# Layer-1 state-space decays: differences of running sums over 24 rows instead of 128-row sums of steps

## The chip, the cores and the metric

The kernel runs on one core of one Trainium2 chip. The metric is device time in microseconds (us) of one execution. The kernel before took 3012.22 us, the median of 18 runs (3007.47 to 3018.83).

## What is computed

The program is a whole decoder of four layers over 32 sequences of 64 tokens (2048 tokens, width 256). Each layer has an attention-like mixer, a cross attention and a feed-forward part. The change touches one of the twelve parts: the mixer of layer 1, a state-space model with 32 heads. Layer 2 has a mixer of the same kind with 8 heads, in the same functions. Cut to what matters, the reference for layer 1 is:

```python
dt = softplus(dt + dt_bias)
A = -exp(A_log)                         # one negative number for each head
dA = exp(dt * A)
def step(h, inp):                       # one step for each token of a sequence
    h = dA_t[:, :, None, None] * h + (dt_t[:, :, None] * x_t)[..., None] * B_t[:, :, None, :]
    y = einsum('bhpn,bhn->bhp', h, C_t)
```

The kernel doesn't walk over the tokens. Over a sequence of 64 tokens the recursion is a masked product: token n adds to the output of token m (m not before n) its input dt·x, weighted by C·B of the two tokens and by a decay, exp(da[n+1] + ... + da[m]) with da = dt·A. All da are negative. So for each head there is a 64x64 matrix of decays, and what the change replaces is how the exponents of these matrices are summed.

## The kernel before, in words

**Tiling.** The tokens lie in 16 tiles of 128 rows; a tile holds two whole sequences. A unit of the mixer (`unit_ssm`, line 1369) takes two tiles, 256 tokens. It normalizes, projects dt and computes da (lines 1380 to 1389; da is 128 rows by 2 tiles by 32 heads), and prepares B, C and their masked product cb. Then `unit_ssm_heads` (line 1401) runs four times for layer 1, with j = 0, 4, 8 and 12, eight heads each (once for layer 2). Such a call is called a block below. Layer 1 has 8 units, so 32 blocks; layer 2 has 8 units, so 8 blocks.

**A block before.** One elementwise product makes `ra` (lines 1411 to 1414): the step da of a row, repeated over 64 columns, kept where the column's token is at or after the row's (`upto`). It is recorded with `combine`, which lets the planner choose VectorE or GpSimd. For each of the two tiles, one matmul of the constant 128x128 matrix `after` with 512 columns of `ra` (line 1421) sums the steps between two tokens, and ScalarE's Exp takes the sum out of PSUM into `m` (line 1422). VectorE multiplies m by cb (line 1423). The rest of the block are the projections and the four-tap convolution (`pair`, `conv`), transposes, 32 small 64x64 products of inputs and decays, the gate, and the output projection, which accumulates in two PSUM banks over the four blocks of a unit.

**Engines.** A float32 matmul shows in the trace as two instructions, each with its weight load. TensorE's array is split when a product has few rows or columns: a product over 32 rows uses one of four row strips (the start partition, 0, 32, 64 or 96, says which). `cross_out` (line 1175) uses all four strips at once.

**The order of the work.** The functions only record operations. A planner (`Order`, line 531, and `in_turns`, line 777) puts them in order for each engine before the program is built: a list scheduler that runs forward and backward in turns and keeps the shortest of its forward plans by its own cost formulas (`duration`, line 467). For TensorE these formulas give a float32 product over 128 rows and 512 columns 0.86 us, and one over at most 32 rows 512 x 0.00053 = 0.27 us; a switch between shapes costs 0.1 us (`SWITCH`). While TensorE is in a split shape, ready products of the same shape that stand near (within 10 us of work, `NEAR`) are preferred. Two streams of stages are woven in one order (`body`, line 2568), in three groups of 8, 6 and 2 tiles, so that layer-1 blocks of a later group stand beside stages of layers 2 and 3 of an earlier one. Buffers come from fixed numbers of slots: ten of 4 KB a row (`b4`, where `ra` lies), sixteen of 2 KB (`b2`), eight PSUM banks (`mm`).

Of the kernel before, what the change touches and what calls it, by code (L numbers as in the profile page):

```python
# [22 lines left out]
AF = mybir.ActivationFunctionType  # L23
ALU = mybir.AluOpType
AX = mybir.AxisListType

P = 128
# [14 lines left out]
def _constants():  # L42

    f = np.float32
    r = np.arange(P)
    c = {}
    c["ident"] = np.eye(P, dtype=f)
    c["ones"] = np.ones((P, P), f)

    c["causal"] = np.where(np.arange(64)[None, :] <= (r % 64)[:, None], 0.0, NEG).astype(f)  # L50

    c["upto"] = ((r % 64)[:, None] <= np.arange(64)[None, :]).astype(f)

    c["after"] = ((r[:, None] > r[None, :]) & (r[:, None] // 64 == r[None, :] // 64)).astype(f)

    c["before"] = (r[:, None] < r[None, :]).astype(f)

    c["strip8"] = ((r[:, None] % 32) // 8 == np.arange(4)[None, :]).astype(f)
    c["strip16"] = ((r[:, None] % 32) // 16 == np.arange(2)[None, :]).astype(f)

    c["parity"] = (r[:, None] // 64 == np.arange(2)[None, :]).astype(f)

    c["unit"] = np.broadcast_to(np.eye(1, 32, dtype=f), (P, 32))
    c["iota"] = np.broadcast_to(np.arange(64, dtype=f), (P, 64))
    main = ((r % 64) < 48).astype(f)
    c["mainT"] = np.zeros((P, P), f)
    c["mainT"][0], c["mainT"][1] = main, 1 - main
    c["row"] = r[:, None].astype(f)

    at = (np.arange(NT)[:, None, None] * P + r[None, :, None]) * 6 + np.arange(6)[None, None, :] - NONE  # L70
    c["parts"] = np.transpose(at, (1, 0, 2)).reshape(P, NT * 6).astype(f)
    c["mhalf"] = np.full((P, 32), -0.5, f)

    inv = f(1.0) / f(500000.0) ** (np.arange(0, 64, 2, dtype=f) / f(64))
    ang = inv[r % 32][:, None] * np.arange(64, dtype=f)[None, :]
    co, si = np.cos(ang).astype(f), np.sin(ang).astype(f)
    c["rope0"] = np.concatenate([co, np.where(r[:, None] // 32 % 2 == 0, -si, si)], 1)
    inv = f(1.0) / f(10000.0) ** (np.arange(0, 8, 2, dtype=f) / f(8))
    ang = (r % 64).astype(f)[:, None] * inv[None, :]
    co, si = np.cos(ang).astype(f), np.sin(ang).astype(f)  # L80
    c["rope3"] = np.concatenate([co, co, -si, si], 1)
    at, parts, n = {}, [], 0
    for k, v in c.items():
        at[k] = (n, n + v.shape[1])
        n += v.shape[1]
        parts.append(v.astype(f))
    return np.ascontiguousarray(np.concatenate(parts, 1)), at


_CONST, _AT = _constants()  # L90


# [110 lines left out]
def bc(ap, axis, n):  # L203

    u = ap.unsqueeze(axis)
    s = list(u.shape)
    s[axis] = n
    return u.broadcast_to(s)
# [11 lines left out]
def split(ap, a, pat="p (a b) -> p a b"):  # L220
    return ap.rearrange(pat, a=a)
# [572 lines left out]
class Net:  # L794
# [41 lines left out]
    def k(self, name):  # L836
        a, b = _AT[name]
        return self.const[:, a:b]

    def tile(self, tag, *shape, dtype=F32, parts=P):  # L840
        self.n += 1
        name = sys._getframe(1).f_code.co_name
        if name in ("w", "w4", "b4", "b2", "tmp", "sm", "mm"):
            name = sys._getframe(2).f_code.co_name
        name = f"{name.removeprefix('unit_')}_{tag}_{self.n}"
        t = Tile(tag, [parts, *shape], dtype, name, "psum" if tag == "mm" else "sbuf")
        dims, n = [], 1
        for c in reversed(shape):
            dims.insert(0, (n, c))
            n *= c  # L850
        return View(t, 0, parts, 0, dims, dtype)
# [517 lines left out]
    def unit_ssm(self, layer, W, nh, g, st):  # L1369

        nc = self.nc
        nx = nh // 2
        wx, wg, wr, wo, par = W
        cw = par["cw"].rearrange("p (c k) -> p c k", k=4)
        upto = self.k("upto")
        hT = self.norm(layer, [2 * g, 2 * g + 1])
        pre = self.tile("pre", 256)
        dt, da, cb = (split(pre[:, a : a + 2 * n], 2) for a, n in ((0, nh), (64, nh), (128, 64)))

        pd = split(self.mm()[:, : 2 * nh], 2)  # L1380
        for t in range(2):
            self.prod(pd[:, t, :], [(hT[:, c, t * P : (t + 1) * P], wr[:, c, 256:]) for c in range(2)])
        e = self.sm(2, nh)
        nc.vector.tensor_tensor(dt, pd, bc(par["dtb"], 1, 2), ALU.add)
        nc.scalar.activation(e, dt, AF.Abs)
        nc.scalar.activation(e, e, AF.Exp, scale=-1.0)
        nc.scalar.activation(e, e, AF.Ln, bias=1.0)
        nc.vector.scalar_tensor_tensor(dt, dt, 0.0, e, ALU.max, ALU.add)
        nc.vector.tensor_tensor(da, dt, bc(par["alog"], 1, 2), ALU.mult)
        BC = self.tmp(2, GT)  # L1390
        self.conv(par, cw, BC, self.pair([wr[:, c] for c in range(2)], 0, hT), nx)

        pc = split(self.mm()[:, :P], 2)
        for t in range(2):
            for b in range(2):
                at = slice(t * P + b * 64, t * P + b * 64 + 64)
                nc.tensor.matmul(pc[64 * b : 64 * b + 64, t, :], BC[:, 0, at], BC[:, 1, at], start=True, stop=True)
        nc.vector.tensor_tensor(cb, pc, bc(upto, 1, 2), ALU.mult)
        st.update(hT=hT, dt=dt, da=da, cb=cb)

    def unit_ssm_heads(self, W, nh, g, j, st):

        nc = self.nc
        nx = nh // 2
        wx, wg, wr, wo, par = W
        cw = par["cw"].rearrange("p (c k) -> p c k", k=4)
        upto = self.k("upto")
        first, last = j == 0, j + 4 == nx
        hT, dt, da, cb = st["hT"], st["dt"], st["da"], st["cb"]

        ra = self.b4(2, 8, 64)
        nc.combine(
            ra, bc(da[:, :, 2 * j : 2 * j + 8], 3, 64), bc(bc(upto, 1, 2), 2, 8), ALU.mult
        )
        xs = self.b4(4, GT)
        for u in range(0, 4, 2):
            self.conv(par, cw, xs[:, u : u + 2, :], self.pair(wx, (j + u) * P, hT), j + u)
        gs, m = self.b4(4, GT), self.b4(2, 8, 64)
        for t in range(2):
            ps = self.mm()  # L1420
            self.prod(ps, [(self.k("after"), ra[:, t])])
            nc.scalar.activation(m[:, t], split(ps, 8), AF.Exp)
        nc.vector.tensor_tensor(m, m, bc(cb, 2, 8), ALU.mult)
        for u in range(0, 4, 2):
            nc.scalar.activation(gs[:, u : u + 2, :], self.pair(wg, (j + u) * P, hT), AF.Silu)
# [1 line left out]
        for t in range(2):  # L1427
            ps = split(self.mm(), 4)
# [39 lines left out]
        for u in range(4):  # L1468
            if u == 3:
                for v in range(4):  # L1470
                    rows = slice(32 * v, 32 * v + 32)
# [1140 lines left out]
```

## Time and profile before

The profiled execution took 3022.26 us; its span on the core is 3020.5 us.

| | |
|---|---|
| median of 18 runs | 3012.22 us |
| profiled execution / its span | 3022.26 / 3020.5 us |
| mean granted TensorE clock | 0.961 |
| TensorE matmul (PE) busy | 2850.1 us, 94% |
| VectorE (DVE) | 2110.1 us, 70% |
| GpSimd (POOL) | 1554.6 us, 51% |
| ScalarE (ACT) | 1509.0 us, 50% |
| HBM traffic | 85 GB/s over the span |

Every instruction has the same line in this profile (L2503, the helper that issues the plan), so the groups are told apart by tiles: `ssm_heads_b` and `ssm_heads_mm` are SBUF and PSUM tiles of a block, `ssm_pre` holds dt, da and cb of a unit, `__init___consts` the constants. A form such as 32*128 32x512 is a matmul that uses 32 rows and 128 columns of the array and streams 512 columns. Matmuls overlap, so the time that a matmul takes from the stream is the distance from its start to the next one's start, and not the duration in its row.

The layer-1 mixer's units stand in three stretches of the span: four units from about 442 to 762 us, three from 1462 to 1772, one from 2318 to 2420.

### The profile page before, as it was taken

The page shows a single profiled execution, that of the slowest core. Times are in us where ns is not written, and L with a number is a line of the kernel's source. Part 1 is how long each engine was busy: PE and PEld are TensorE (multiplying, and loading weights), DVE is VectorE, ACT ScalarE, POOL GpSimd, SP SyncE. Part 2 cuts the span into 40 slices and gives each one's busy share as a digit, 9 for nine tenths or more (in the row PEclk, how much of TensorE's full clock was granted, in tenths as well). Part 3 has the DMA queues.
Part 4 walks back from the last instruction along what each step waited for, and adds up shares of the span by engine and source line. Part 5 has one row for each costly group of instructions (what it writes and reads, how often), then busy time and mean ns, then how long its engine had stood idle before and what let it go on. Part 6 is the DMA issues. An engine that isn't in the chain of part 4 may idle for free.

```text
span 3020.5 us, 66624 instructions
## 1 busy us (share of the span) xinstructions
PE 2850.1 (94%) x26612; PEld 2355.5 (78%) x26612; DVE 2110.1 (70%) x5110; ACT 1509.0 (50%) x2842; POOL 1554.6 (51%) x1323
## 2 busy tenths in 40 slices
PE   8999999999998999999999999998899999987667
PEld 7888888777787888888887788777778788866446
DVE  5773548766677667765899987777457889877434
ACT  5552226565444454634666656654326565664330
POOL 6761243234655455326674566665333685465445
PEclk8999999999999999999999999998999999988878
DMA  4012511301531344121010010123561231212424
GB/s 166 16 47 84 181 58 29 138 2 46 211 137 43 93 163 156 54 70 46 29 34 28 26 44 16 69 79 112 192 222 50 73 103 52 87 36 76 139 90 132
DMA packets 120313, 258.90 MB, mean 86 GB/s; under 512 B 27077, under 2 KB 81880, under 8 KB 107588
## 3 DMA queue, kind: packets, MB, share of 16 engines
q1 hardware_dynamic: 110212, 230.54, 22.5%
q0 software_dynamic: 9792, 24.10, 2.3%
q8 instruction: 211, 3.46, 0.5%
q14 instruction: 98, 0.80, 0.1%
HBM read 179.24 MB, written 78.77 MB: 85 GB/s over the span
## 4 chain that ended last, share of the span: by engine, by line
PE 52%; DVE 6%; issue 3%; ACT 2%; POOL 1%; another core or an unknown queue 0%; POOLq 0%; ACTq 0%; DVEq 0%
PE L_xattn_mm L2503 7%; PE pair_mm L2503 6%; PE ssm_heads_mm L2503 5%; PE cross_out_mm L2503 5%; PE L_ffn_mm L2503 4%; PE L_attn_mm L2503 3%; PE L_block_mm L2503 3%; PE turn_mm L2503 2%; PE heads_mm L2503 2%; PE L_dense_mm L2503 2%; PE L_experts_mm L2503 2%; PE small_scores_mm L2503 2%; PE outrows_mm L2503 1%; PE L_expert_mm L2503 1%; PE small_values_mm L2503 1%
## 5 line engine op out<-in xcount | busy, mean ns | idle before, releaser
L2503 PE MATMUL pair_mm<-norm_b,load_ssm_w 128*128 128x256 f32 x1280 | 304.5, 381 | 1.4 <-ACT ssm_heads_b L2503 0.8
L2503 PEld LDWEIGHTS pair_mm<-norm_b,load_ssm_w 128*128 128x128 f32 x1280 | 236.3, 190 | 40.8 <-issue 8.3
L2503 DVE SCALAR_TENSOR_TENSOR ssm_heads_b<-pair_mm,load_ssm_wp,ssm_heads_b 128x252 f32<-128x252 f32 (+2 forms) x480 | 196.4, 465 | 26.0 <-ACT ssm_heads_b L2503 24.7
L2503 POOL TENSOR_TENSOR L_xattn_sm<-L_xattn_sm,__init___consts 128x8 f32<-128x8 f32 (+2 forms) x64 | 188.1, 2944 | 26.0 <-DVE L_xattn_sm L2503 19.8
L2503 POOL TENSOR_TENSOR norm_sm<-norm_sm,__init___consts 128x1 f32<-128x1 f32 (+1 forms) x149 | 94.7, 641 | 207.0 <-DVE norm_sm L2503 177.7
L2503 ACT ACT_TABLE_LOAD x151 | 193.7, 1283 | 9.2 <-PE ssm_heads_mm L2503 2.8
L2503 ACT COPY rope_b<-rope_mm 32x512 f32<-32x512 f32 x238 | 137.0, 576 | 121.8 <-DVE rope_b L2503 78.9
L2503 ACT COPY L_xattn_b<-L_xattn_mm 128x512 f32<-128x512 f32 x170 | 99.9, 591 | 163.8 <-PE L_xattn_mm L2503 149.8
L2503 PE MATMUL rope_mm<-norm_b,load_L_attn_w 128*128 128x128 f32 x1280 | 169.3, 289 | 5.1 <-ACT rope_b L2503 3.0
L2503 PEld LDWEIGHTS rope_mm<-norm_b,load_L_attn_w 128*128 128x128 f32 x1280 | 161.8, 203 | 12.8 <-issue 6.3
L2503 PE MATMUL ssm_heads_mm<-load_ssm_w,ssm_heads_b 128*128 128x256 f32 x640 | 165.2, 391 | 0.2 <-POOL ssm_heads_b L2503 0.2
L2503 ACT COPY turn_b<-turn_mm 128x512 f32<-128x512 f32 x192 | 106.1, 595 | 76.1 <-PE turn_mm L2503 71.6
L2503 PEld LDWEIGHTS ssm_heads_mm<-load_ssm_w,ssm_heads_b 128*128 128x128 f32 x640 | 115.9, 191 | 33.5 <-issue 18.4
L2503 POOL TENSOR_TENSOR rope_b<-rope_b,__init___consts 128x512 f32<-128x512 f32 x74 | 82.3, 1113 | 99.4 <-ACT rope_b L2503 71.0
L2503 ACT COPY norm_b<-norm_mm 128x256 f32<-128x256 f32 (+1 forms) x139 | 58.7, 437 | 143.2 <-PE norm_mm L2503 118.9
L2503 DVE TENSOR_SCALAR norm_b<-__init___x,norm_sm,norm_sm 128x256 f32<-128x256 f32 x192 | 110.1, 590 | 26.4 <-POOL norm_sm L2503 10.7
L2503 PEld LDWEIGHTS L_xattn_mm<-norm_b,load_L_xattn_w 128*128 128x128 f32 x1024 | 120.3, 192 | 7.7 <-issue 6.1
L2503 POOL TENSOR_TENSOR ssm_heads_b<-ssm_heads_b,ssm_heads_b 128x1024 f32<-128x1024 f32 x33 | 80.5, 2444 | 88.4 <-DVE ssm_heads_b L2503 64.2
L2503 PE MATMUL cross_out_mm<-load_L_xattn_w,cross_out_b 128*128 128x256 f32 x512 | 124.5, 389 | 0.0
L2503 PE MATMUL L_xattn_mm<-norm_b,units_L_xattn_w 128*128 128x128 f32 x1024 | 121.8, 276 | 2.8 <-issue 2.8
L2503 PE MATMUL L_xattn_mm<-norm_b,load_L_xattn_w 128*128 128x128 f32 x1024 | 124.3, 276 | 0.0
L2503 POOL TENSOR_TENSOR L_xattn_b<-L_xattn_b,shift_sm 128x1024 f32<-128x1024 f32 x30 | 58.1, 1937 | 128.3 <-DVE shift_sm L2503 108.3
(434 smaller groups left out, 7954.2 us busy)
## 6 DMA issues: line engine op xcount, KB each, us to landing
L_block_w<-in_f_rows SPq DMA_DIRECT2D x42, 770.0 KB
queue<-far_w SPq DMA_DIRECT2D x14, 1024.0 KB
load_ssm_w<-in_s_in SPq DMA_DIRECT2D x12, 1024.0 KB
parts<-far_w SPq DMA_DIRECT2D x10, 1024.0 KB
slots<-far_w SPq DMA_DIRECT2D x16, 548.0 KB
L_experts_b<-slots SPq DMA_DIRECT2D x32, 274.0 KB
units_L_xattn_w<-kept_x SPq DMA_DIRECT2D x8, 1024.0 KB
L_parts_b<-parts SPq DMA_DIRECT2D x14, 512.0 KB
```

Of the source, the lines that this page charges most:

```text
L2503: done = getattr(getattr(nc, e), method)(*map(real, op.args), **kw)
```

## The change

For layer 1 alone (nx == 16), the exponent is made as a difference of running sums. Once for a unit, da is spread over 128 columns (four strips of 32: in a strip 8 heads in each of four kinds: first sequence, second sequence, both, none), and for each tile one matmul of this spread with 192 constant columns (`upto` and `within`) gives the running sums. Two tiles are then built from the sums in PSUM: `lo` (128 rows by 2 by 128) and `hi` (128 rows by 2 by 8 by 64, a `b4` slot). In a block j, the product over rows 8j to 8j+24 of `lo` and `hi` is running sum at m minus running sum at n: 24 rows, in strip j/4. The two products of a block lie in the same strip; the four blocks of a unit lie in four different strips. Above the diagonal the difference has the wrong sign and could be large, so ScalarE takes it from PSUM with Relu of the negated value, and a third activation makes the exponentials of all 1024 columns from SBUF. Layer 2's blocks stay as they were. The cost formulas of the planner and the stages' costs are unchanged.

```diff
+    c["within"] = ... # 128 columns
+    c["kinds"] = ...  # 4
+    c["side"] = ...   # 128
+    c["floor"] = ...  # 2
+    c["own"] = ...    # 8
...
 unit_ssm
         nc.vector.tensor_tensor(da, dt, bc(par["alog"], 1, 2), ALU.mult)
+        rows = None
+        if nx == 16:
+            sp = self.tmp(2, 4, 4, 8)
+            for t in range(2):
+                nc.vector.tensor_tensor(
+                    sp[:, t], bc(split(da[:, t], 4), 2, 4), bc(bc(self.k("kinds"), 1, 4), 3, 8), ALU.mult
+                )
+            pc = self.mm()[:, :384].rearrange("p (t n) -> p t n", t=2)
+            for t in range(2):
+                self.prod(pc[:, t], [(sp[:, t].rearrange("p a b c -> p (a b c)"), self.both("upto", "within"))])
+            lo, hi = self.tmp(2, P), self.b4(2, 8, 64)
+            fl = self.k("floor")
+            nc.vector.scalar_tensor_tensor(lo, pc[:, :, 64:], fl[:, 1:2], bc(self.k("side"), 1, 2), ALU.mult, ALU.add)
+            for t in range(2):
+                nc.vector.scalar_tensor_tensor(
+                    hi[:, t], bc(pc[:, t, :64], 1, 8), fl[:, 0:1], bc(self.k("own"), 2, 64), ALU.max, ALU.mult
+                )
+            rows = lo, hi
...
 unit_ssm_heads
-        ra = self.b4(2, 8, 64)
-        nc.combine(
-            ra, bc(da[:, :, 2 * j : 2 * j + 8], 3, 64), bc(bc(upto, 1, 2), 2, 8), ALU.mult
-        )
+        rows = st["rows"]
+        if not rows:
+            ra = ... # as before
...
             ps = self.mm()
-            self.prod(ps, [(self.k("after"), ra[:, t])])
-            nc.scalar.activation(m[:, t], split(ps, 8), AF.Exp)
+            if rows:
+                r = slice(8 * j, 8 * j + 24)
+                self.prod(ps, [(rows[0][r, t], rows[1][r, t].rearrange("p h n -> p (h n)"))])
+                nc.scalar.activation(m[:, t], split(ps, 8), AF.Relu, scale=-1.0)
+            else:
+                ... # as before
+        if rows:
+            nc.scalar.activation(m, m, AF.Exp, scale=-1.0)
         nc.vector.tensor_tensor(m, m, bc(cb, 2, 8), ALU.mult)
```

The new constants add 270 columns to a tile of 1145 that is loaded at the start.

More of the change, by code (lines that the diff above doesn't have):

```diff
@@ L52, in _constants @@
     c["upto"] = ((r % 64)[:, None] <= np.arange(64)[None, :]).astype(f)
+    kind = r[:, None] % 32 // 8
+    half = np.arange(P)[None, :] // 64
+    c["within"] = np.where((r[:, None] // 64) == half, (r[:, None] % 64) <= (np.arange(P)[None, :] % 64), False).astype(f)
     c["after"] = ((r[:, None] > r[None, :]) & (r[:, None] // 64 == r[None, :] // 64)).astype(f)
+    c["kinds"] = np.concatenate([r[:, None] < 64, r[:, None] >= 64, r[:, None] >= 0, r[:, None] < 0], 1).astype(f)
+    c["side"] = ((kind == half) & (kind < 2)).astype(f)
+    c["floor"] = np.concatenate([np.where(kind == 2, 1.0, -3e38), np.where(kind == 2, -1.0, 0.0)], 1).astype(f)
+    c["own"] = ((r[:, None] % 8 == np.arange(8)[None, :]) & (kind < 3)).astype(f)
     c["before"] = (r[:, None] < r[None, :]).astype(f)
@@ L838, in k, with both @@
         return self.const[:, a:b]
+    def both(self, a, b):
+        return self.const[:, _AT[a][0] : _AT[b][1]]
     def tile(self, tag, *shape, dtype=F32, parts=P):
@@ L1398, in unit_ssm @@
         nc.vector.tensor_tensor(cb, pc, bc(upto, 1, 2), ALU.mult)
-        st.update(hT=hT, dt=dt, da=da, cb=cb)
+        st.update(hT=hT, dt=dt, da=da, cb=cb, rows=rows)
     def unit_ssm_heads(self, W, nh, g, j, st):
@@ L1409, in unit_ssm_heads @@
         hT, dt, da, cb = st["hT"], st["dt"], st["da"], st["cb"]
-        ra = self.b4(2, 8, 64)
-        nc.combine(
-            ra, bc(da[:, :, 2 * j : 2 * j + 8], 3, 64), bc(bc(upto, 1, 2), 2, 8), ALU.mult
-        )
+        rows = st["rows"]
+        if not rows:
+            ra = self.b4(2, 8, 64)
+            nc.combine(
+                ra, bc(da[:, :, 2 * j : 2 * j + 8], 3, 64), bc(bc(upto, 1, 2), 2, 8), ALU.mult
+            )
         xs = self.b4(4, GT)
@@ L1420, in unit_ssm_heads @@
             ps = self.mm()
-            self.prod(ps, [(self.k("after"), ra[:, t])])
-            nc.scalar.activation(m[:, t], split(ps, 8), AF.Exp)
+            if rows:
[3 more added lines that the diff above has]
+            else:
+                self.prod(ps, [(self.k("after"), ra[:, t])])
+                nc.scalar.activation(m[:, t], split(ps, 8), AF.Exp)
+        if rows:
+            nc.scalar.activation(m, m, AF.Exp, scale=-1.0)
         nc.vector.tensor_tensor(m, m, bc(cb, 2, 8), ALU.mult)
```

## The prediction

> **What bounds the kernel now.** I read the totals and the slices first, then the three stretches where the layer-1 mixer runs, then the chain of waits in the weakest of them, then groups by form, then single rows of the timeline.
>
> ```profile
> PE 2850.1 (94%) x26612; PEld 2355.5 (78%) x26612; DVE 2110.1 (70%) x5110; ACT 1509.0 (50%) x2842; POOL 1554.6 (51%) x1323
> 442.00:762.00 320.00, 319.17 (x2717) 256.50 (x2716) 223.98 (x546) 186.12 (x296) 116.86 (x79) 1.00 0.14 51
> 1462.00:1772.00 310.00, 306.90 (x3123) 248.91 (x3123) 280.60 (x709) 197.93 (x355) 177.45 (x148) 1.00 0.11 35
> 2318.00:2420.00 102.00, 102.00 (x934) 80.58 (x934) 80.40 (x194) 64.45 (x120) 63.41 (x39) 1.00 0.19 66
> ```
>
> The last three are the stretches of the 4, 3 and 1 layer-1 units: length, then busy time of PE, PEld, DVE, ACT and POOL, the granted clock (1.00), DMA share and GB/s. TensorE is busy for 728 of 732 us, so in these stretches a microsecond of TensorE work is a microsecond of the kernel, and work of ScalarE (about 61%) and GpSimd is covered. VectorE is covered in the first and third stretch (70 and 79%); in the second it has 90%, and the chain of waits there runs partly over it:
>
> ```profile
> by line: PE pair_mm L2503 25.2%; PE ssm_heads_mm L2503 19.8%; PE L_xattn_mm L2503 5.4%; DVE fp_b L2503 5.4%; PE turn_mm L2503 4.3%; POOL L_xattn_sm L2503 4.0%; DVE ssm_heads_b L2503 3.8%; PE small_values_mm L2503 3.7%; PE L_attn_mm L2503 3.
> ```
>
> So TensorE decides, and the question is what a 24-row product costs against one of 128 rows.
>
> **The main products.** Timeline rows (start, length, engine, instructions):
>
> ```profile
> 475.44 1.88 PE L2503 MATMUL ssm_heads_mm<-ssm_heads_b,__init___consts 128*128 128x512 f32 x4
> 477.16 0.38 PE L2503 MATMUL L_ffn_mm<-load_L_ffn_w,L_ffn_b 128*128 128x256 f32 x1
> ...
> 2960.72 2.11 PE L2503 MATMUL L_dense_mm<-norm_b,load_L_experts_w 128*128 128x256 f32 x9
> 2962.75 2.85 PE L2503 MATMUL L_dense_mm<-L_dense_b,d_L_experts_w 32*128 32x256 f32 x12
> 2965.53 1.13 PE L2503 MATMUL L_dense_mm<-load_L_ffn_ws,L_ffn_b 64*128 64x256 f32 x4
> ...
> 269.83 2.02 PE L2503 MATMUL cross_out_mm<-blocks_b,context_cx 32*128 32x512 f32 x16
> ```
>
> The first is a block's pair of products now: 4 instructions, 477.16 - 475.44 = 1.72 us to the next start, 0.43 us each; 32 blocks take 55 us. In the second group 9 full-array instructions of 256 columns take 2.03 us to the next start, 12 in one 32-row strip 2.78 us: 0.226 and 0.232 us each. **Rows that aren't used save nothing: a strip streams its columns as slowly as the whole array.** Only the last row shows a gain: 16 instructions of 512 columns in 2.02 us, with four strips at work, where 16 x 0.43 would be 6.9. The change puts both products of a block in one strip, so a block alone still takes 1.72 us.
>
> The Trainium skill ("TensorE: Matmul & The Clock Gate", section "Why this matters for your kernels") states that a single product over 32 rows takes as long as one over 128, and that only products in distinct row groups run together, 3.07 times as fast for four. By its factor, with four strips always filled, the 55 us would shrink by an estimated 37 us; by its first half they don't shrink at all. The strip rows above agree with that first half.
>
> **What the split shape adds.** By the first group 256 columns take 0.43 / 2 = 0.215 us, so the nine take 1.94 of their 2.03 us and 0.09 goes into changing shape; the twelve take 2.58 of 2.78, and 0.20 goes. One visit to the split shape costs 0.29 us. If each block makes one visit, 32 x 0.29 = +9.3 us. Bounds: 0 (beside another split shape, where the change is paid already) and twice that, if the two tiles' products are issued apart.
>
> **The sums once for a unit.** 2 products x 2 instructions x 192 columns, at 0.43/512 us a column: 0.65 us, x 8 units = +5.2 us of TensorE.
>
> **What strips may give back.** The strips of a unit are filled at once only if products of two blocks stand side by side. All eight of a unit can start as soon as lo and hi are there, and the order now does bring blocks near each other:
>
> ```profile
> 600.41 1.02 PE L2503 MATMUL ssm_heads_mm<-ssm_heads_b,__init___consts 128*128 128x512 f32 x2
> 601.27 0.60 PE L2503 MATMUL ssm_heads_mm<-__init___consts,ssm_heads_b 128*128 128x128 f32 x4
> 601.71 1.02 PE L2503 MATMUL ssm_heads_mm<-ssm_heads_b,__init___consts 128*128 128x512 f32 x2
> 602.57 0.59 PE L2503 MATMUL pair_mm<-norm_b,load_ssm_w 128*128 128x256 f32 x2
> 603.16 1.10 PE L2503 MATMUL ssm_heads_mm<-ssm_heads_b,__init___consts 128*128 128x512 f32 x2
> ```
>
> Three products in 3.6 us; one more follows at 608.33. In each of the first four units two of the four blocks come within some 10 us, and the planner prefers a near product of the same split shape. I take one meeting of two blocks for each unit: 8. A meeting saves one visit (0.29) and between nothing and all of the second block's 1.72 us: each strip's own products go one after the other, and how far the second strip runs ahead in the queue no row shows. I take half, 0.86: 8 x 1.15 = -9.2 us. Bounds: 0 meetings, and 16 (every block meets another) with full overlap, 16 x 2.01 = -32.
>
> TensorE in sum: 9.3 + 5.2 - 9.2 = **+5.3 us**.
>
> **The other engines.**
>
> ```profile
> L2503 POOL TENSOR_TENSOR ssm_heads_b<-ssm_pre,__init___consts 128x1024 f32<-128x1024 f32 x34 | 67.2, 1985 | 86.3 <-PE ssm_heads_mm L2503 35.1 <-DVE ssm_heads_b L2503 17.6 <-DVE ssm_pre L2503 15.5
> L2503 ACT ACTIVATE ssm_heads_b<-ssm_heads_mm 128x512 f32<-128x512 f32 x80 | 44.6, 597 | 18.7 <-PE ssm_heads_mm L2503 18.3
> L2503 ACT ACTIVATE heads_b<-heads_b 128x1024 f32<-128x1024 f32 x64 | 67.1, 1065 | 12.2 <-POOL heads_b L2503 10.9 <-DVE heads_b L2503 1.1
> ```
>
> - Removed: 32 of `ra`, 29 on GpSimd (the row above holds layer 2's too): 29 x 1.985 = 57.6 us, and 3 on VectorE. GpSimd isn't the bound; nothing is gained directly.
> - VectorE added for a unit: two spreads (128 elements; `ssm_pre<-ssm_mm` of that size 0.28 us), lo (the 128x256 `__init___x<-ssm_heads_mm`, 0.476 us) and two halves of hi (512 from PSUM: 0.682 us for a product of two, some 0.07 more with a scalar operand, as 0.476 stands to 0.411 at 256): 2.54 us, x 8 = 20.3 us.
> - ScalarE: two Relu of the size that the two Exp had (0.597 us), plus one Exp of 1024 from SBUF: 1.065 x 32 = 34 us more. No Relu is in the trace; Identity stands between two Silu there without a table load (455.4 to 457.5 us), so I take none for Relu. With two loads a block, 2 x 1.283 us, ScalarE would have 10% more to do, still covered.
> - Of these, what counts is the second stretch: VectorE 3 x 2.54 = 7.6 us and ScalarE 12 x 1.065 = 12.8 us, 20.4 together. Its 12 `ra` were all on GpSimd, so VectorE saves none there. 13.2% of the chain there is named as VectorE's or GpSimd's: **+2.7 us**. Bounds: -6.5 (a VectorE product of 1024 takes 1.75 us beside a GpSimd one and 1.22 alone; 12 x 0.54 comes back) and +20.4.
> - The multiply by cb now waits for Relu and a longer Exp. Behind it on VectorE stand the next convolution steps, and TensorE waits for m in the 64x64 products; with 728 of 732 us busy it has other work then. Nothing taken; it is in the +20.4.
> - hi holds one of ten `b4` slots for a whole unit (some 60 us); `ra` held one four times for a unit (three made at 515.9 to 519.6 us were used from 521 to 564). I take no difference.
> - The first GpSimd step waits for the constants, issued at 1.20 us and landed at 5.66. 270/1145 = 24% more bytes: **+0.7 us**, bounds 0 and 1.05. No DMA is moved past another.
>
> **Sum:** 5.3 + 2.7 + 0.7 = +8.7 us. The profiled execution took 3022.3 (span 3020.5, 1.8 around it), 10 above the median of the runs; on it 3031.0, on the median 3012.2 + 8.7 = **3021 us**.
>
> **Rivals.**
>
> *Strips filled (faster).* Every block meets another and fully overlaps: 9.3 + 5.2 - 32 + 3.4 = -14 us, 2998. For it: the products are all ready at once and near ones are preferred. Against it: a free PSUM bank for each (two of eight hold the output sums), and 20 us of other work between two blocks in the first stretch (320 us / 16).
>
> *No strips meet.* 9.3 + 5.2 + 3.4 = +18 us, 3030. For it: transposes and projections lie between the products in the rows above. The change then doesn't do what a product over strips is for.
>
> *The second stretch turns to VectorE (slower).* Price: all of the 20.4 us, with meetings as in my forecast: 5.3 + 20.4 + 0.7 = +26 us, 3039. It decides once VectorE's idle time there (310 - 281 = 29 us) can't take the added 20 us of it and ScalarE's longer chain. Against it: TensorE is idle for only 3 us there now.
>
> **Chances.** Forecast (some meetings, partial overlap) 42%, within some 7 us; filled strips 21%; no meetings 22%; VectorE's stretch 15%. About 0.2%, 6 us, can be told from no change. Faster by more: 0.03 + 0.17 = 0.20. Within: 0.12 + 0.04 + 0.01 = 0.17. Slower: 0.27 + 0.21 + 0.15 = 0.63. The planner orders the whole program anew, so the idle time elsewhere falls anew too; I give it no sign. Range 2998 to 3041; the likeliest case alone 3014 to 3028.
>
> **What would show it.** Right: 24-row instructions of 512 columns 0.43 us apart within a strip, 0.09 to 0.1 more around them; 32 Relu pairs, 32 Exp of 1024; GpSimd 57 us lighter; TensorE near 100% in the three stretches. Wrong: 24-row instructions of several strips starting within hundredths of a microsecond of each other in most units (then faster), or 24-row products faster than 0.43 us alone, or idle TensorE over 10 us in the second stretch.

## The result, and the profile after

The changed kernel takes **3060.29 us**, the median of 8 runs (3053.68 to 3069.78); the kernel before, run beside it and earlier 50 times in all, has a median of 3013.65. The ratio is **1.0157, with an interval of 1.0143 to 1.0170**: 47 us slower, where +9 was forecast and the range ended at +29. The profiled execution after took 3052.05 us (span 3050.3), 8 below its median; that of before was 9 above its own. So the two profiles differ by 30 us only, and 17 of the 47 are in no pair of traces that can be laid side by side.

The totals of the page after, and the three stretches that the prediction read (length; busy PE, PEld, DVE, ACT, POOL; granted clock; DMA share; GB/s):

```profile
PE 2882.3 (94%) x26652; PEld 2370.6 (78%) x26652; DVE 2142.4 (70%) x5157; ACT 1524.4 (50%) x2844; POOL 1522.2 (50%) x1312
```

```profile
442.00:762.00 320.00, 318.31 (x2702) 255.46 (x2701) 226.03 (x541) 191.31 (x300) 90.75 (x62) 0.98 0.15 54
1462.00:1772.00 310.00, 303.75 (x3033) 244.61 (x3031) 271.78 (x711) 196.43 (x344) 139.13 (x137) 0.99 0.11 35
2318.00:2420.00 102.00, 100.59 (x948) 81.20 (x947) 82.21 (x210) 65.93 (x112) 46.61 (x30) 0.98 0.16 55
```

Two things to see. TensorE is still busy for 723 of 732 us (728 before), and no other engine came nearer to being the bound: VectorE has 88% in the second stretch, less than its 90% before. And the granted clock, 1.00 in all three stretches before, is 0.98, 0.99 and 0.98. A busy TensorE at a lower clock looks like a full one in the share; 0.02 x 320 + 0.01 x 310 + 0.02 x 102 = 11.5 us are lost in these windows alone. That column stood beside the numbers that I read, and the prediction has no term for it.

The groups that the change made or shrank (busy us, mean ns, idle before):

```profile
L2541 PE MATMUL ssm_heads_mm<-ssm_b,ssm_b 24*128 24x512 f32 x128 | 49.0, 628 | 0.4 <-DVE ssm_heads_b L2541 0.4
L2541 PE MATMUL ssm_mm<-__init___consts,ssm_b 128*128 128x192 f32 x32 | 6.7, 328 | 0.0
L2541 POOL TENSOR_TENSOR ssm_heads_b<-ssm_pre,__init___consts 128x1024 f32<-128x1024 f32 x7 | 13.7, 1962 | 15.7 <-DVE ssm_pre L2541 9.7 <-PE L_attn_mm L2541 4.3 <-DVE norm_sm L2541 1.5
```

The products over strips in the timeline of after (start, length, instructions):

```profile
471.13 1.99 PE L2541 MATMUL ssm_heads_mm<-ssm_b,ssm_b 24*128 24x512 f32 x10
473.05 0.45 PE L2541 MATMUL ssm_mm<-ssm_b 128*64 128x64 f32 x8
```

```profile
593.48 2.06 PE L2541 MATMUL ssm_heads_mm<-ssm_b,ssm_b 24*128 24x512 f32 x8
595.46 0.44 PE L2541 MATMUL ssm_heads_mm<-__init___consts,ssm_heads_b 128*128 128x128 f32 x2
```

```profile
617.90 2.89 PE L2541 MATMUL ssm_heads_mm<-ssm_b,ssm_b 24*128 24x512 f32 x4 [0.38 <-DVE ssm_heads_b L2541]
620.72 3.32 PE L2541 MATMUL ssm_heads_mm<-ssm_heads_b,ssm_heads_b 64*64 64x64 f32 x64
623.97 0.42 PE L2541 MATMUL ssm_mm<-load_ssm_ws,norm_b 128*128 128x32 f32 x1
```

In the first pair ten instructions of three strips take 1.92 us to the next start, in the second two whole blocks take 1.98: strips do overlap where blocks meet, and instructions of two or three blocks run side by side in 10 of the 25 visits. In the third a block stands alone, its four instructions take 2.82 us, and the 64 small products behind it take 3.25. In a place at full clock these 64 take 1.84 us (shown below). The clock was halved at 618.8 us, in the middle of the block.

**A measure for what follows.** Each kernel's order is different, so I cut each span at the same progress of TensorE: where it has issued 16 to 28%, 52.5 to 64% and 80 to 84% of the matrix work that the change leaves as it was. These three parts hold the units of layer 1, with a few blocks of layer 2 between them, and their lengths can be compared. In them: the length, TensorE's time for the decay products (those of layer 2 there included) and for the sums once for a unit (start to next start, without the excess at half clock), the time at half clock, and idle time of TensorE, all in us, worked out from the trace's rows; the last column is the rest of the span. The lengths depend on how the work is weighed; weighed by rows, columns and streamed length, their differences between kernels are right within some 3 us. The idle column is no copy of the profile's: by the busy time above, TensorE is idle for 4 us in the three stretches before and for 9 after.

| kernel | three parts | decay products | unit sums | at half clock | idle | rest of the span |
|---|---|---|---|---|---|---|
| before | 750.1 | 60.8 | 0 | 0 | 17.7 | 2270 |
| after | 767.2 | 49.8 | 5.4 | 23.9 | 26.2 | 2283 |
| after, profiled again | 776.4 | 49.8 | 5.4 | 44.4 | 26.6 | 2280 |

So of the 30 us (36 in the second profile of after) 17 (26) lie in these parts, and 13 (10) elsewhere. Before's parts hold one more of layer 2's blocks than after's; layer 1's own decay products took 55.7 us before and take 46.2 after.

### The profile page after: what moved, and what is told of

Read it like the earlier page. It is cut to its first block, busy times and chain, and to the rows that moved or that the text cites. A ratio compares the mean times of both kernels' runs of the same rounds, so it can differ in the third digit from the quotient of the medians.

```text
span 3050.3 us, 66705 instructions
## 1 busy us (share of the span) xinstructions
PE 2882.3 (94%) x26652; PEld 2370.6 (78%) x26652; DVE 2142.4 (70%) x5157; ACT 1524.4 (50%) x2844; POOL 1522.2 (50%) x1312
## 5 line engine op out<-in xcount | busy, mean ns | idle before, releaser
L2541 DVE SCALAR_TENSOR_TENSOR ssm_heads_b<-pair_mm,load_ssm_wp,ssm_heads_b 128x252 f32<-128x252 f32 (+2 forms) x480 | 196.0, 466 | 20.2 <-ACT ssm_heads_b L2541 19.0
L2541 ACT ACT_TABLE_LOAD x149 | 191.2, 1283 | 10.6 <-PE L_ffn_mm L2541 3.3
L2541 PE MATMUL rope_mm<-norm_b,load_L_attn_w 128*128 128x128 f32 x1280 | 161.4, 280 | 12.1 <-ACT L_attn_b L2541 2.8
L2541 PEld LDWEIGHTS rope_mm<-norm_b,load_L_attn_w 128*128 128x128 f32 x1280 | 154.2, 195 | 20.4 <-issue 6.4
L2541 ACT ACTIVATE ssm_heads_b<-ssm_heads_b 128x1024 f32<-128x1024 f32 (+1 forms) x152 | 124.2, 831 | 49.9 <-DVE ssm_heads_b L2541 21.8
L2541 POOL TENSOR_TENSOR rope_b<-rope_b,__init___consts 128x512 f32<-128x512 f32 x75 | 96.5, 1290 | 91.5 <-DVE rope_b L2541 53.2
L2541 POOL TENSOR_TENSOR heads_b<-heads_b,heads_sm 128x1024 f32<-128x1024 f32 x52 | 99.9, 1933 | 57.5 <-DVE heads_sm L2541 49.8
L2541 PE MATMUL L_attn_mm<-load_L_attn_w,L_attn_b 128*128 128x256 f32 x512 | 123.1, 385 | 0.0
```

The source lines that it names most:

```text
L2541: done = getattr(getattr(nc, e), method)(*map(real, op.args), **kw)
```

## The experiments

Five theories. **A**: the added operations cost what they cost where they stand. **B**: the planner made a new order of the whole program, and it is a worse one. **C**: the planner's low price for a 24-row product, 0.27 us, misleads it. **D**: ScalarE's longer chain (Relu, Relu, Exp of 1024) isn't covered. **E**: the added steps of TensorE and VectorE cost it, and the slot that `hi` holds; in the last runs, the strips' own price. In the first eight runs every kernel, the one before too (2899 to 2901 us), was some 4% faster; only ratios are compared with those.

### Orders exchanged and drawn anew

To carry an order over, every operation is marked, the planner plans one version of the program, and the other version is emitted in that order:

```diff
-    issue(tc, in_turns(net.nc.ops, Net.SLOTS, 120.0, net.spare, 4), Net.SLOTS)
+PLAN_NEW, EMIT_NEW, KEEP = False, True, (7,)    # new_on_old
+PLAN_NEW, EMIT_NEW, KEEP = True, False, ()      # old_on_new
```

In the first, seven of the eight units are changed and the last stays as before. For the redrawn orders one number of the planner's search, the 120.0, becomes 117, 119, 121 or 123, and nothing else changes.

> The changed computation in the order that was planned for the kernel before: each product, each activation and each multiply stands where its counterpart stood, the sums of a unit come some 6 us ahead of their first use, and buffers are handed out anew along that order. The last of the eight units keeps the old form, since no slot is free there for hi. Theory A (the added operations themselves cost the time: shape changes, VectorE, ScalarE's longer chain): 25 to 45 us over the kernel before, 3040 to 3060. Theory B (the new order of the whole program costs it, the operations next to nothing): within 8 us of the kernel before, 3006 to 3022.

> The computation of before in the order that was planned for the changed kernel; ra is made on GpSimd 6 us ahead of its first product in that order. Theory A (the operations cost): back to 3013 to 3025. Theory B (the order costs): stays at 3045 to 3062.

> The kernel before, planned with a look-ahead of 121 us where it had 120: the same operations, only another order. Theory B in its strong form (the order of before was a lucky one among its neighbours, so that any new order costs): 15 to 40 us over before, 3028 to 3053. If order has little to do with it: within 8 us, 3005 to 3022.

> The changed kernel, planned with a look-ahead of 123 us where it had 120: only another order. Theory A: as the changed kernel, 3050 to 3070. Theory B: anywhere from 3020 to 3075, and not where the changed kernel is.

> The kernel before, planned with a look-ahead of 117 us where it had 120: only another order. Theory B in its strong form (a lucky order before): 3028 to 3053. If order has little to do with it: 3005 to 3022.

> The changed kernel, planned with a look-ahead of 119 us where it had 120: only another order. Theory A (the operations cost): 3050 to 3070. Theory B (the order costs): anywhere from 3020 to 3075.

Measured: new_on_old 1.0233 (1.0215 to 1.0251), old_on_new 1.0339 (1.0320 to 1.0358). Both far slower, and since even the unchanged operations lose 3.4% in a carried order, the pair told mostly the price of the carrying itself, in which all buffers are handed out anew. It was done better below. The redrawn orders: before_h121 1.0016 (1.0006 to 1.0026), before_h117 1.0073 (1.0048 to 1.0099); after_h123 1.0175 (1.0158 to 1.0192), after_h119 1.0137 (1.0114 to 1.0159). Three orders of before lie within 0.73%, three of after (1.0157, 1.0175, 1.0137) above all of them. The loss isn't one unlucky order, but an order alone moves this kernel by up to 22 us.

### The planner's price, and two strips for a block

```diff
+            if args[1].n == 24:
+                return n * 0.00167 + 0.004
```

```diff
-                r = slice(8 * j, 8 * j + 24)
+                a = 8 * (j + 8 * t) % 128
+                r = slice(a, a + 24)
```

The first tells the planner 0.86 us, as for 128 rows. The second puts the two products of a block into two strips (with the columns of the spread exchanged to match, in two VectorE steps for the second tile).

> The changed kernel, planned with the price that the trace shows for a 24-row product alone (512 columns 0.86 us instead of 0.27). Theory C (the planner is misled by the low price and packs the layer-1 stretches too tightly): 20 us or more off the changed kernel, 3020 to 3040. Theories A and B: no systematic gain, 3045 to 3075.

> The changed kernel with the second tile's heads turned by two blocks when they are spread, so that the two products of a block lie in two different strips and can run beside each other. Their pair should take about 0.9 us to the next start where one strip takes 1.73, so 32 x 0.85 = 27 us less of TensorE, of which some 5 us were had already by blocks that met. Theory A: 22 us below the changed kernel, about 3038, with 15 either way for the new order under theory B.

true_cost 1.0122 (1.0093 to 1.0151): 4 us below after_h119, the intervals overlap. Theory C falls as the main cause. two_strips 1.0090 (1.0066 to 1.0114): by the ratios 20 us better than the changed kernel, where 22 were expected, and 14 to 25 better than its two redrawn orders. In the three parts its decay products take 33.8 us in place of 49.8, it has 17.1 us at half clock, and the parts are 747.9 us long, no longer than before's. It computes the reference, and is the best changed version found; it doesn't beat the kernel before. It is a single drawn order, and a draw alone moves a kernel by up to 22 us.

### ScalarE's part and the constants

exp_direct drops the Relu and the third activation (together called the clamp below):

```diff
-                nc.scalar.activation(m[:, t], split(ps, 8), AF.Relu, scale=-1.0)
+                nc.scalar.activation(m[:, t], split(ps, 8), AF.Exp, scale=0.001)
...
-        if rows:
-            nc.scalar.activation(m, m, AF.Exp, scale=-1.0)
```

before_relu adds the same three activations to layer 1 of the kernel before, and before_pad only 270 columns of constants:

```diff
+            nc.scalar.activation(m[:, t], split(ps, 8), AF.Relu if nx == 16 else AF.Exp, scale=-1.0 if nx == 16 else 1.0)
+        if nx == 16:
+            nc.scalar.activation(m, m, AF.Exp, scale=-1.0)
```

```diff
+    c["pad"] = np.zeros((P, 270), f)
```

> The changed kernel as it is, beside the other three on one chip. Both theories: 1.3 to 1.8% over before, as it was.

> The changed kernel with ScalarE's part as it was: Exp straight from PSUM, no Relu and no third activation. The Exp is taken of a thousandth of the difference, so that it stays finite above the diagonal; the decays that come out are not those of the reference. Theory D (ScalarE's longer chain, 34 us more of it, is what the change costs): 20 us or more below the changed kernel, 1.000 to 1.008 of before. Theory E (VectorE's and TensorE's added steps and the held slot cost it): 1.010 to 1.018.

> The kernel before with ScalarE's part of the change alone: Relu of the negated sum from PSUM and a third activation, Exp of 1024 from SBUF (the same decays where the mask keeps them: the sums are not positive). Theory D (ScalarE's longer chain costs it): 20 us or more, 1.008 to 1.016 of before. Theory E: within 10 us, 0.998 to 1.004, the scatter of a new order included.

> The kernel before with 270 unused columns added to the constants: the bigger load at the start, and every later buffer at another address; operations and order are those of before. If neither matters: within 3 us, 0.999 to 1.002. If the addresses or the load are what costs outside the layer-1 stretches: 20 us or more, 1.006 to 1.012.

after_again 1.0154 (1.0132 to 1.0176). exp_direct **0.9931** (0.9909 to 0.9953): 70 us below it, and faster than before. before_relu 1.0057 (1.0041 to 1.0074), between what the two theories gave; before_pad 1.0016 (1.0003 to 1.0030). The 70 us looked like proof of theory D, yet two things spoke against it: the same work added to before cost 0.57%, 17 us, not 70, and 17 is within what a new order alone does; and of exp_direct's span, 2986 us, the three parts took 750.4 and the rest 2236, against 776.4 and 2280 in after_again. 44 of the 70 us came where the change has no work. Each of these kernels had drawn an order of its own. So the next runs hold the order still.

### The order held

Here the big buffers alone (three kinds of SBUF slots) are handed out anew, all PSUM banks are those of before, and the order of every engine is that of before; where the changed kernel has an operation in place of another, it stands there. As in new_on_old, seven of the eight units are changed.

```diff
+PLAN_NEW, EMIT_NEW, KEEP = False, False, ()     # old_on_old2
+PLAN_NEW, EMIT_NEW, KEEP = False, True, (7,)    # new_on_old2, direct_on_old2
```

direct_on_old2 has the Exp of a thousandth of exp_direct. exp_direct_h123 is exp_direct with the 120.0 as 123.

> The operations of the kernel before in its own order, with the buffers of the layer-1 blocks handed out anew by the same rule as in the next two kernels. If the order decides (theory B), this is within 0.5% of the kernel before (0 to +15 us), and it is the base for the next two. If the handing out of the buffers is what made the two earlier kernels with a carried order slow, it is over 1% slower (+30 us or more).

> The changed operations in the order of the kernel before: each new operation stands where the one that it replaces stood, and all PSUM and weight buffers are those of before. If the added work of ScalarE costs by itself (theory D), this is 15 to 35 us slower than the run before it in this set, and most of that comes in the three layer-1 stretches. If the new order of the whole program costs (theory B), it is within 6 us of that run.

> The run before with one exponential of a thousandth of the sums on each tile in place of the clamp of each tile and the exponential of both (the decays are not the reference's). Theory D: 10 us faster to 5 us slower than the carried order without the change, since TensorE's products are shorter and ScalarE has no more work than before. Theory B: no more than 6 us from the run before it.

> The kernel without the clamp (one exponential of a thousandth of the sums on each tile, the decays are not the reference's) with a second draw of the order, a horizon of 123 in place of 120. Theory D: within 0.6% of the kernel before (-25 to +18 us), as the first draw was at -0.7%, and at least 25 us faster than the changed kernel at the same horizon (1.0175). Theory B: the first draw was luck, and this one is 1.0% or more slower than before (+30 us).

| kernel | ratio to before (interval) | three parts | decay products | at half clock | idle | rest of the span |
|---|---|---|---|---|---|---|
| old_on_old2 | 1.0125 (1.0098 to 1.0153) | 749.3 | 60.9 | 0 | 16.9 | 2282 |
| new_on_old2 | 1.0212 (1.0189 to 1.0234) | 781.7 | 66.4 | 17.1 | 23.6 | 2294 |
| direct_on_old2 | 1.0222 (1.0200 to 1.0243) | 775.0 | 66.2 | 10.2 | 20.2 | 2302 |
| exp_direct | 0.9931 (0.9909 to 0.9953) | 750.4 | 44.2 | 13.7 | 21.0 | 2236 |
| exp_direct_h123 | 1.0088 (1.0059 to 1.0118) | 746.2 | 41.1 | 10.2 | 23.4 | 2288 |

The handing out alone costs 1.25%, the second of the outcomes named: it explains a good part of what made the first pair of carried orders slow, and is the base here. Over it the changed operations cost 0.87%, 26 us (give or take 11), within the 15 to 35 that theory D gave. But **taking the clamp away gives nothing back** (1.0222 against 1.0212; theory D wanted the carried order's own time or better), though the three parts did get 7 us shorter. And exp_direct's second order is 1.6% slower than its first: 47 us between two orders of one program, as much as the whole result. In the three parts, where the change works, the two agree within 5 us. So in the held order D falls, and the 70 us were for the greater part a lucky order. In the orders that the program drew itself D isn't settled: without the clamp the three parts take 750.4 and 746.2 us, as long as before's 750.1 and 17 to 30 less than after's, with less time for decay products (44.2 and 41.1 us for 49.8) and at half clock (13.7 and 10.2 for 23.9 and 44.4).

### The strips taken away, with every order and buffer kept

```diff
+                nc.ops[-1].full = rows[0][:, t], rows[1][:, t].rearrange("p h n -> p (h n)")
...
+            if full:
+                op.args = (op.args[0], *full)
```

The planner sees the strip, the chip gets the product over all 128 rows.

> The changed operations in the order of before, buffers and order of every engine as in that run, but each product of layer 1 covers all 128 rows of the two operands in place of 24 (so it adds the four blocks' sums together, and the decays are not the reference's). If the strips cost (theory E): 20 to 30 us faster than that run: 5 of the products, 11 of the changes to a strip's shape, 5 to 12 of the windows at half clock, and no dip of the clock in the first two layer-1 stretches. If the cost lies with what VectorE, ScalarE and GpSimd do, it is within 6 us of it.

> The changed kernel, order and buffers of every engine unchanged, with each product of layer 1 over all 128 rows (the four blocks' sums are added together, the decays are not the reference's). The products lose their meetings (about 9 us more of TensorE), and the changes to a strip's shape (7 us) and the half-clock windows behind strips (10 to 17 us) go. Theory E, the strips' own price: 5 to 20 us faster than the changed kernel. Theory D, ScalarE's longer chain: 0 to 10 us slower than it, since only the loss of the meetings shows.

after_full **1.0116** (1.0098 to 1.0133), 12 us (give or take 7) below the changed kernel (1.0154 and 1.0157; the medians, 3042.74 and 3057.40, say 15), although its blocks can't meet in strips any more and its decay products take 60.8 us for 49.8. full_on_old2 1.0186 (1.0169 to 1.0203), 8 us below new_on_old2 by the ratios and 13 by the medians (3064.10, 3076.72): less than the 20 to 30 expected, and the intervals touch.

The two kernels of a pair issue the same matmuls in the same order, so the start of each can be compared, and the gain has a place. In the held order full_on_old2 gains 17.7 us in the three regions of layer 1 (440 to 770, 1460 to 1800 and 2320 to 2440 us) and loses 2 elsewhere. The rows account for most of it: 5.4 us of layer 1's decay products (54.1 and 48.7), 0.09 us ahead of each of the 40 visits, and 6.8 us of clock. In the drawn order it is otherwise: against the two profiles of after, after_full gains -1.4 and 6.2 us in these regions, since it loses 11 us of meetings there, and 8.8 and 8.0 us between 1800 and 2320 us. No strip stands there; TensorE is at half clock for 17 and 24 us less, and no run shows why. So in the held order theory E's price shows where the strips stand, and in the drawn one most of the 12 us lies elsewhere.

The mechanism can be seen in one place. A lone visit in after_again, and the same step of the program in after_full:

```profile
603.26 1.98 PE L2541 MATMUL ssm_heads_mm<-ssm_b,ssm_b 24*128 24x512 f32 x4
605.17 2.85 PE L2541 MATMUL ssm_heads_mm<-ssm_heads_b,ssm_heads_b 64*64 64x64 f32 x64
607.96 1.97 PE L2541 MATMUL ssm_heads_mm<-__init___consts,ssm_heads_b 128*128 128x1 f32 x8
```

```profile
608.55 1.88 PE L2545 MATMUL ssm_heads_mm<-ssm_b,ssm_b 128*128 128x512 f32 x4
610.36 1.91 PE L2545 MATMUL ssm_heads_mm<-ssm_heads_b,ssm_heads_b 64*64 64x64 f32 x64
612.20 0.60 PE L2545 MATMUL ssm_heads_mm<-__init___consts,ssm_heads_b 128*128 128x1 f32 x4
```

The products themselves cost nearly the same, 1.91 and 1.81 us to the next start. The 64 small ones behind them take 2.79 us after the strip and 1.84 after the full array. The stretches around both, after_again first (the columns as above; the clock is third from the end):

```profile
602.36:605.77 3.41, 3.41 (x34) 1.56 (x28) 1.29 (x2) 2.37 (x4) 0.00 (x0) 1.00 0.00 0
605.77:612.60 6.83, 6.83 (x67) 6.17 (x63) 3.49 (x12) 3.80 (x5) 0.86 (x2) 0.50 0.01 2
612.60:616.01 3.41, 3.41 (x17) 2.98 (x17) 1.45 (x2) 0.00 (x0) 1.94 (x2) 1.00 0.00 0
```

```profile
605.20:608.61 3.41, 3.41 (x26) 2.52 (x25) 2.10 (x3) 0.21 (x1) 0.00 (x0) 1.00 0.00 0
608.61:612.02 3.41, 3.41 (x67) 2.17 (x67) 0.83 (x2) 2.74 (x4) 0.00 (x0) 1.00 0.00 0
612.02:615.43 3.41, 3.25 (x28) 2.86 (x23) 2.53 (x7) 3.08 (x4) 0.70 (x1) 1.00 0.02 5
```

TensorE is busy for 3.41 of 3.41 us ahead of the drop, so it wasn't waiting; it was streaming through 24 of 128 rows for 1.91 us of them, and the next 6.83 us ran at half clock, 3.4 us lost. With full rows nothing drops here. (The three stretches of after_full aren't laid on the grid on which its clock steps, 606.38, 609.79 and so on; on it the full product is cut in two, so this pair alone doesn't separate the rows from the place on the grid.)

All windows of the grid together do. For each window of 3.41 us at full clock, in the traces of before, after, after_again, after_full, new_on_old2 and full_on_old2, an estimate of the used share of the array can be made from the rows: rows x columns of each matmul over 128 x 128, for the time that its columns stream at 0.43 us for 512. Of 4606 windows with a share over 0.40 none is followed by half clock; under 0.35 it is 194 of 206, and between the two 21 of 79. In 33 of these 215 windows TensorE was busy for over 95% of the time. The window at 602.36 us in after_again has 0.35; with its 24-row products counted as 128 rows it would have 0.76.

Over the three regions of layer 1, after_again, after_full, before, and then new_on_old2 and full_on_old2 (for the last three without the third region, where the clock is 1.00 in each):

```profile
440.00:770.00 330.00, 328.08 (x2735) 262.84 (x2735) 231.17 (x557) 196.63 (x309) 93.07 (x65) 0.97 0.14 53
1460.00:1800.00 340.00, 333.74 (x3222) 269.06 (x3222) 290.32 (x744) 215.79 (x381) 157.84 (x154) 0.97 0.10 32
2320.00:2440.00 120.00, 118.59 (x1070) 93.34 (x1069) 99.17 (x249) 77.65 (x134) 63.80 (x42) 0.99 0.17 58
```

```profile
440.00:770.00 330.00, 328.01 (x2789) 262.58 (x2789) 233.86 (x558) 197.73 (x310) 93.60 (x65) 1.00 0.14 53
1460.00:1800.00 340.00, 333.89 (x3350) 271.61 (x3349) 295.34 (x752) 219.76 (x387) 161.59 (x154) 0.99 0.11 35
2320.00:2440.00 120.00, 116.59 (x1126) 92.06 (x1126) 94.56 (x227) 77.13 (x147) 68.97 (x42) 0.98 0.21 70
```

```profile
440.00:770.00 330.00, 329.17 (x2790) 264.25 (x2789) 231.06 (x559) 190.38 (x305) 118.76 (x83) 1.00 0.14 49
1460.00:1800.00 340.00, 336.56 (x3556) 274.77 (x3555) 306.24 (x762) 216.89 (x392) 198.34 (x164) 1.00 0.10 32
```

```profile
440.00:770.00 330.00, 328.57 (x2692) 252.45 (x2691) 224.57 (x561) 192.03 (x301) 82.62 (x64) 0.99 0.13 49
1460.00:1800.00 340.00, 332.63 (x3154) 264.84 (x3153) 293.59 (x755) 214.49 (x379) 165.29 (x154) 0.98 0.11 35
```

```profile
440.00:770.00 330.00, 328.10 (x2768) 264.55 (x2767) 231.33 (x571) 199.40 (x313) 90.82 (x68) 1.00 0.13 49
1460.00:1800.00 340.00, 332.53 (x3295) 269.75 (x3295) 297.46 (x766) 219.26 (x389) 165.67 (x153) 0.99 0.11 35
```

The clock's loss is 0.03 x 330 + 0.03 x 340 + 0.01 x 120 = 21 us in after_again and 3.4 + 2.4 = 6 in after_full; 3.3 + 6.8 = 10 and 3.4 in the two of the held order; none in before. Within each pair the busy times of VectorE and ScalarE differ by at most 7.4 us in a region, so those engines do much the same. Of the time at half clock in the three parts, after_full keeps 10.2 us of 44.4 (23.9 in the first profile of after), and full_on_old2 3.4 of 17.1.

## Why the prediction was wrong

- **The main products: right.** Four instructions of 24 rows take 0.53 and then 0.43 us each to the next start, and a lone block 1.9 us.
- **What the split shape adds: the step that failed.** "One visit to the split shape costs 0.29 us", the prediction has it, from rows of the dense stage. The change of shape was right: 0.09 us on the instruction ahead, 0.10 on the first and 0.09 on the last of the 24-row products, at 25 visits where 24 were forecast (32 less 8 meetings). But a visit also lowers the use of the array for 2 us, and the clock answers in the next 3.4 to 10 us. The prediction has no term for that. By the granted clock the regions of layer 1 lose 11.5 to 21 us in the two profiles of after, of which after_full keeps 6. With the strips taken away and all else kept, these regions are 1.4 us longer and 6.2 shorter than in the two profiles of after, though 11 us of meetings are lost: outside its own products a visit cost (11 - 1.4) / 25 and (11 + 6.2) / 25, with the 0.19 within them 0.6 and 0.9 us, two to three times the forecast. The Trainium skill ("TensorE: Matmul & The Clock Gate", section "What's actually happening") describes a free-running window of 3413 ns and a clock that goes to half after an idle window; the window's length agrees with the 3.41 and 6.83 us here, but in the place shown TensorE wasn't idle, so the measurement goes further than the page.
- **Sums for a unit: right** (5.4 us for +5.2). **Meetings: right** in size (layer 1's decay products -9.5 us, the change of shape within them included, for -9.2).
- So TensorE's own sum, forecast +5.3, was -9.5 + 5.4 + 25 x 0.09 = -1.9 us at full clock, and +10 to +20 with the clock. In the three parts it was the clock and not the array's time that decided.
- **The other engines: mis-sized.** Forecast +2.7 in the second stretch alone. TensorE's idle time in the three parts rose by 8.5 us (17.7 to 26.2; 5.4 by the profile's busy time in the three stretches), and by 7.7 in the held order with full rows (16.9 to 24.6); that is within the bound of +20.4. The held order gives the sum of all that isn't strips, unit sums included: full_on_old2 less old_on_old2, 0.61% or 18 us (give or take 10), of which 14.7 lie in the three parts (749.3 to 764.0). ScalarE's own share: in the held order taking the clamp away gave nothing back. In the second region (1460 to 1800 us) of after, ScalarE's two longest waits are these (us in total, times, longest):

```profile
ACT ssm_heads_b L2541 <- PE ssm_heads_mm L2541: 30.1, 19, 5.1
ACT ssm_heads_b L2541 <- PE pair_mm L2541: 27.1, 17, 4.9
```

  They were 20.6 and 17.4 before: ScalarE waits for TensorE longer than it did. TensorE's own waits for ScalarE in that region are 3.0 us, 1.5 before, none of them for a block's decays. "Covered" fits this, and the held order by direct_on_old2. In the orders that the program drew itself, the kernels without the clamp were 70 and 26 us faster; how much of that is the clamp and how much the draw stays open.
- **Relu without table loads: right** (149 loads after, 151 before). **GpSimd:** `ra` went from 34 products to 7, but the total fell by 32 us and not by 57, since the planner gave it other products.
- **Constants:** +0.7 with a bound of 1.05; before_pad, which also moves every later buffer, measured 0.16%, 5 us, interval 1 to 9. Too low, by little.
- **Rivals.** *Strips filled* was half right about the products and came out on the other side. *No strips meet* holds in the carried order (decay products +5.5 us, 40 visits). *VectorE's stretch* didn't happen: TensorE is idle for 6.3 us in the second stretch, where over 10 would have shown it, and VectorE is less busy than before. None of the three had the clock or a new order, and the range ended some 20 us short.
- **"The idle time elsewhere falls anew; I give it no sign."** It is 10 to 13 us of the profiles' difference, in places where the change has no work. The planner's order is the likeliest reason, though no run shows it alone: two orders of exp_direct differ by 47 us, three of before by 22. It belonged in the range as a width, some 20 us to each side; at zero width the range was too narrow even without the clock.

**The 47 us in sum.** In the three parts the two profiles of after are 17 and 26 us longer than before. The rows account for this within some 3 us: layer 1's decay products -9.5, the sums once for a unit +5.4, the change of shape ahead of the visits +2.3, the half clock +12 and +22, idle time +8.5 and +8.9. In the held order the same parts grew by 32.4 us (749.3 to 781.7), 17.7 of it the strips' and 14.7 all else's. The other 30 and 21 of the 47 lie where the change has no work. The order that the planner drew, the slots that it handed out and the clock there come into question; no run separates them, since a carried order costs 1.25% by itself, and this part of the cause stays open.

## What to carry to other kernels

Where TensorE is the bound, read the granted clock beside the busy share: a product over a few rows can be paid a second time, in the clock of what comes behind it, so small-row products belong together in filled strips or not in the dense stretches at all. Where a planner orders the whole program, hold the order and the buffers and change one operation, as the last two runs do; two orders of the same program can differ by as much as the effect. And give such a redraw a width in the forecast, taken from a few redrawn orders of the kernel before.

## What was unexpected of the hardware

- The clock steps in windows of 3.41 us on a fixed grid: in the six traces named above, every drop of the clock begins and ends on it, within 0.03 us. In the regions of layer 1, after has 5 drops and after_again 7; 2 and 5 of them come right behind a window that holds 24-row products. These seven windows use 0.18 to 0.35 of the array, and with 128 rows would use 0.50 to 0.95. Not every one of the 25 visits is followed by a drop: most windows with a visit stay over 0.40, since the grid cuts the visit in two or fuller products stand beside it. A few of 0.31 to 0.39 aren't followed by one either, so the estimate draws no sharp line.
- Two products in one strip go one after the other (0.43 us each); in different strips they start 0.01 us apart, also when they are instructions of three different blocks.
- The first 24-row instruction of a visit takes 0.53 us, and the last 0.52 until the next shape starts.
- In the first eight runs the kernel before took 2899 to 2901 us, in the others 3010 to 3014: 4%, with similar ratios (1.0137 and 1.0175 for the redrawn orders of the changed kernel there, 1.0154 for the changed kernel here). It isn't shown to be the chip: the chips are numbered 4 and 6 there, and 5 and 6 in the later runs. Single instructions take the same in before and before_h121 (1283 ns a table load, 381 ns a product of `pair`), and no run shows where the difference comes from.
